# Where LayerNorm's inverse root is computed: a power on GpSimd, or a logarithm and an exponential on ScalarE

## The chip, the cores and the metric

The kernel runs on one core of a Trainium2 chip. A core has five engines that run side by side, each with its own queue of instructions taken in order: TensorE (PE; its weight loads are PEld), VectorE (DVE), ScalarE (ACT), GpSimd (POOL) and SyncE (SP), which here starts the DMA transfers. An instruction that needs what another engine makes waits for a semaphore, and all that stands behind it on its engine waits too. The metric is the time of one execution on the device, in microseconds (us), lower is better; the median of several runs is compared.

## The reference, cut to what matters

Two transformer layers with adaptive layer norm act on `x` of 16 sequences, 512 tokens and 256 channels. Each layer is a token mixer and a channel mixer, each behind a LayerNorm that is scaled and shifted per sequence, and each added back through a gate:

```python
def _layernorm(x, axis=-1, eps=1e-05):
    m = jnp.mean(x, axis=axis, keepdims=True)
    v = jnp.var(x, axis=axis, keepdims=True)
    return (x - m) / jnp.sqrt(v + eps)
...
    h = _layernorm(x, axis=-1) * (1 + ca) + sa
    x = x + ga * _L0_attn_ref(h, ...)          # fast weights: a recurrence over chunks of 16 tokens
    h = _layernorm(x, axis=-1) * (1 + cb) + sb
    x = x + gb * _L0_ffn_ref(h, ...)           # low-rank MLP with GELU
    ...
    h = _layernorm(x, axis=-1) * (1 + ca) + sa
    x = x + ga * _L1_attn_ref(h, ...)          # attention in a window of 64, and 4 global keys
    h = _layernorm(x, axis=-1) * (1 + cb) + sb
    x = x + gb * _L1_ffn_ref(h, ...)           # channel mix: squared ReLU, gated by a sigmoid
```

So there are four LayerNorms for every token. The change bears on 1 / sqrt(v + eps) in each.

## The kernel before, in words

**Units.** The 16 sequences are split in two halves of 8, and the 512 tokens in 8 blocks of 64. A half and a block make a unit, 16 in all, and the two halves take turns. A unit is a tile `x` of 128 partitions (two sequences of 64 tokens) by 4 rows of 256 channels.

**Stages.** Each unit goes through five generators: `prepare` (norm `a`, projections, convolutions and SiLU, the results spilled to memory), `chain` (the recurrence of the fast weights, four chunks of 16 tokens in a unit, `recur`), `mlp` (the end of the fast weights, then `low_rank_ffn` with norm `b` and GELU), `attend` (`window_attention` with norm `c`) and `mix` (`channel_mix` with norm `d`). The letters stand in the names of tiles: `mv_a`, `rs_a`, `off_a` and `xn_a` belong to the norm of `prepare`.

**The order of work.** The function `timetable` gives each step of each generator a due time, and the steps of all units are emitted in order of it, so five stages of several units are interleaved. A scheduler then plans, from its own estimates, the order in which each engine takes its instructions; the program is fixed before it runs. Bursts of tanh, SiLU and GELU on ScalarE go through `run`, which keeps a burst together where it can and then loads the table of the logarithm and exponential again (L234). That table, `natural_log_exp_and_others`, is the resident one between bursts.

**The recurrence.** In `recur`, VectorE makes scores from tokens and state (`sc_k`, `sc_v`, L527, and their sums, L528), ScalarE takes exponentials (L542, L613), VectorE normalises (L547 to L549, L619 to L623), GpSimd makes outer products of 128x1024 (`pd_o`, `pd_i`, `pd_kv`, L534 and L661), and VectorE sums them (L636) or scans them (L631). The state lies in PSUM. The two halves' recurrences run side by side, and a chunk starts from the state that the last one left.

**The norm.** `norm_T` (L340 on) is called 64 times, once per stage and unit:

- VectorE: statistics of each of 4 rows, `bn_stats` and `bn_aggr` (L347, L348), into `mv`, mean and variance of 128 x 4 tokens;
- GpSimd: variance plus eps (L350), and that to the power -0.5 (L351, with `mhalf`, a constant of -0.5), into `rs`;
- VectorE: `off` = -mean x `rs` (L353);
- ScalarE: `xn` = x times `rs` plus `off`, one activation for each row (L359);
- TensorE transposes `xn` (L361) into `pt`, and ScalarE scales and shifts it out of there, eight activations of 128x64 for every two rows (L367), into `hT`.

So each norm goes from VectorE to GpSimd, back to VectorE, and on to ScalarE. What stands behind `off` on VectorE and behind `xn` on ScalarE waits with them. Other places take inverse roots by logarithm and exponential on ScalarE already (`inverse_root`, L203 and L204), on tiles of 128x32.

Of the kernel before, what the change touches and what calls it, by code (L numbers as in the profile page):

```python
# [12 lines left out]
AF = mybir.ActivationFunctionType  # L13
ALU = mybir.AluOpType
# [3 lines left out]
P = 128  # L18
# [5 lines left out]
NR = HB // 2  # L24
# [10 lines left out]
EPS = 1e-5  # L35
# [60 lines left out]
def adaln_blocks(ctx: ExitStack, tc: tile.TileContext, a: dict, out: bass.AP):  # L96
    nc = tc.nc
    mul, add, sub = ALU.mult, ALU.add, ALU.subtract
# [9 lines left out]
    def ctile(shape, name):  # L108
        return const.tile(shape, F32, tag=name, name=name)

    def bank(name):
        return ps.tile([P, 512], F32, tag="bank", name=name)
# [75 lines left out]
    nc.vector.tensor_copy(ident_bf, ident)  # L188

    w_proj = ctile([P, 2, 2, C], "w_proj")  # L190
    mhalf = ctile([P, 1], "mhalf")
    nc.vector.memset(mhalf, -0.5)

    def hold(dst, n):

# [144 lines left out]
    def norm_T(x, layer, which, b0, tag, hT):  # L340


        m = mods[layer]
        mv = work.tile([P, NR, 2], F32, tag=f"mv_{tag[0]}", name=f"mv_{tag}", bufs=1)
        for r in range(NR):
            st = work.tile([P, 6], F32, tag="st", name=f"st_{tag}_{r}", bufs=4)
            nc.vector.bn_stats(st, x[:, r, :])  # L347
            nc.vector.bn_aggr(mv[:, r, :], st)  # L348
        rs = work.tile([P, NR], F32, tag=f"rs_{tag[0]}", name=f"rs_{tag}", bufs=1)
        nc.gpsimd.tensor_scalar(rs, mv[:, :, 1], EPS, None, add)  # L350
        nc.gpsimd.tensor_tensor(rs, rs, mhalf.to_broadcast([P, NR]), ALU.pow)  # L351
        off = work.tile([P, NR], F32, tag=f"off_{tag[0]}", name=f"off_{tag}", bufs=1)
        nc.vector.scalar_tensor_tensor(off, mv[:, :, 0], -1.0, rs, mul, mul)  # L353
        for r2 in range(NR // 2):
            pt = bank(f"pt_{tag}_{r2}")
            for n in range(2):
                r = 2 * r2 + n
                xn = work.tile([P, C], F32, tag="xn", name=f"xn_{tag}_{r}", bufs=2)
                nc.scalar.activation(xn, x[:, r, :], AF.Identity, scale=rs[:, r : r + 1], bias=off[:, r : r + 1])  # L359
                for k in range(2):  # L360
                    nc.tensor.transpose(pt[:, (2 * n + k) * P : (2 * n + k + 1) * P], xn[:, k * P : (k + 1) * P], ident)  # L361
            for n in range(2):
                for k in range(2):
                    for e in range(2):
                        b = 4 * r2 + 2 * n + e
                        col = (2 * n + k) * P + e * TB
                        nc.scalar.activation(  # L367
                            hT[:, k, b, :],
                            pt[:, col : col + TB],
                            AF.Identity,  # L370
                            scale=m[:, 2 * which + 1, k, b0 + b : b0 + b + 1],
                            bias=m[:, 2 * which, k, b0 + b : b0 + b + 1],
                        )
            yield
# [35 lines left out]
    def prepare(u):  # L410
# [7 lines left out]
        x = load_x(u, f"xa{u}", "xa", 1)  # L418
        hT = hidden("a", f"hTa{u}")
        yield from norm_T(x, 0, 0, b0, f"a{u}", hT)  # L420
        hf = [hT[:, k].rearrange("p b t -> p (b t)") for k in range(2)]

# [295 lines left out]
    def low_rank_ffn(i, x):  # L718
        b0 = place(i)[0] * HB
        hT = hidden("b", f"hTb{i}")  # L720
        yield from norm_T(x, 0, 1, b0, f"b{i}", hT)
        pp = bank(f"pP{i}")
        for k in range(2):
# [46 lines left out]
    def window_attention(i, x):  # L770
# [4 lines left out]
        far, last = tb > 1, tb == T // TB - 1  # L775
        hT = hidden("c", f"hTc{i}")
        yield from norm_T(x, 1, 0, b0, f"c{i}", hT)
        hf = [hT[:, k].rearrange("p b t -> p (b t)") for k in range(2)]

# [415 lines left out]
```

## Time and profile before

| | before |
|---|---|
| median of 3 runs | 3226.88 us (3222.9 to 3235.52) |
| the profiled execution | 3231.29 us, of which the span from first to last instruction 3229.5 us |
| VectorE busy | 2395.3 us, 4513 instructions |
| TensorE busy (ends modelled) | 2385.4 us, 17232 matmuls |
| ScalarE busy | 1783.6 us, 3748 instructions, 232 of them table loads of 1283 ns |
| GpSimd busy | 1673.0 us, 1575 instructions |
| granted TensorE clock | 0.822 of full speed |

The profile is of one execution. "Busy" counts an instruction from its start to its end. A row of a group reads: line, engine, operation, the tile written and the tiles read, shape, how often; then busy us and the mean ns of one; then the idle time of the engine just before these instructions and what ended it. The chain of waits is followed back from the last instruction, at each step to what released it.

### The profile page before, as it was taken

How to read it: one execution, taken by the hardware profiler on the slowest of the kernel's cores; microseconds unless marked ns; L12 is line 12 of the kernel's file. 1: busy time of each engine (PE TensorE's matmuls, PEld its weight loads, DVE VectorE, ACT ScalarE, POOL GpSimd, SP SyncE). 2: the span in 40 equal slices, each digit the busy share in tenths (PEclk: the TensorE clock that was granted, in tenths of full speed). 3: DMA queues.
4: the chain of work that ended last, by engine and by line, in shares of the span. 5: the costliest groups of instructions: out<-in, count | busy, mean ns of one | idle time of the engine just before them, and what ended most of it. 6: DMA issues, size and time to landing. Idle time of an engine off the chain costs nothing.

```text
span 3229.5 us, 47324 instructions
## 1 busy us (share of the span) xinstructions
PE 2385.4 (74%) x17232; PEld 1452.9 (45%) x17232; DVE 2395.3 (74%) x4513; ACT 1783.6 (55%) x3748; POOL 1673.0 (52%) x1575
## 2 busy tenths in 40 slices
PE   3540156868787776887788887889787888788996
PEld 2210123444444454554445554555445555555664
DVE  1688787878787787778888888888888878774221
ACT  1761354556665745565564666566664655445543
POOL 0245556556556655555556564555555655654112
PEclk7775676878797887888888798979888887879998
DMA  5420112132314132131313223230402212122010
GB/s 151 94 58 13 47 37 67 31 73 55 80 36 94 32 83 54 51 83 33 88 27 72 69 59 75 51 83 27 100 21 72 62 51 56 45 52 60 17 28 27
DMA packets 439307, 186.46 MB, mean 58 GB/s; under 512 B 323937, under 2 KB 413090, under 8 KB 439074
## 3 DMA queue, kind: packets, MB, share of 16 engines
q1 hardware_dynamic: 439074, 183.44, 23.2%
q8 instruction: 135, 2.21, 0.3%
q14 instruction: 98, 0.80, 0.1%
HBM read 116.66 MB, written 66.72 MB: 57 GB/s over the span
## 4 chain that ended last, share of the span: by engine, by line
DVE 33%; PE 22%; POOL 20%; ACT 12%; issue 8%; DMA 4%; SPq 1%; POOLq 0%; DVEq 0%; ACTq 0%
POOL pd_o L534 5%; POOL pd_i L534 4%; DVE pd_kv L631 4%; DVE sc_v L527 3%; POOL pd_kv L534 3%; DVE sv L528 3%; DVE do L636 2%; PE st L873 2%; DVE di L636 2%; DVE sc_k L527 2%; DVE pp L460 2%; PE pproj L1005 2%; DMA oT<-o 2%; DVE scs L528 2%; DVE mx L889 1%
## 5 line engine op out<-in xcount | busy, mean ns | idle before, releaser
L534 POOL TENSOR_TENSOR pd_o<-e_k,dt_v 128x1024 f32<-128x1024 f32 x128 | 301.0, 2358 | 171.4 <-DVE e_k L549 171.3
L534 POOL TENSOR_TENSOR pd_i<-e_v,dt_k 128x1024 f32<-128x1024 f32 x128 | 298.4, 2369 | 43.4 <-DVE e_v L549 43.4
L708 PE MATMUL pwo<-w_WoT,oT 128*128 128x256 f32 x256 | 106.6, 576 | 223.0 <-POOL oT L701 201.8
L873 PE MATMUL st<-qs,keys 32*128 32x128 f32 x2048 | 191.3, 336 | 71.7 <-DVE yT L983 29.0
L661 POOL TENSOR_TENSOR pd_kv<-hid,pd_kv 128x1024 f32<-128x1024 f32 x64 | 150.3, 2349 | 165.6 <-DVE fw L632 141.6
L873 PE MATMUL sc<-keys,qs 32*128 32x128 f32 x2048 | 183.1, 326 | 71.7 <-DVE mx L889 41.7
L636 DVE TENSOR_REDUCE do<-pd_o 128x64 f32<-128x1024 f32 x126 | 152.3, 1213 | 102.5 <-POOL pd_o L534 102.5
L636 DVE TENSOR_REDUCE di<-pd_i 128x64 f32<-128x1024 f32 x128 | 155.1, 1214 | 88.3 <-POOL pd_i L534 88.3
L873 PEld LDWEIGHTS st<-qs,keys 32*128 32x128 f32 x2048 | 160.5, 226 | 132.2 <-DVE mx L889 32.4
L873 PEld LDWEIGHTS sc<-keys,qs 32*128 32x128 f32 x2048 | 148.0, 216 | 141.9 <-DVE mx L889 58.8
L889 DVE TENSOR_REDUCE mx<-sc 128x4 f32<-128x512 f32 x256 | 168.2, 679 | 26.2 <-PE sc L870 26.2
L708 PEld LDWEIGHTS pwo<-w_WoT,oT 128*128 128x128 f32 x256 | 68.4, 287 | 250.7 <-POOL oT L701 218.3
L534 POOL TENSOR_TENSOR pd_kv<-hid,dt_v 128x1024 f32<-128x1024 f32 x64 | 151.4, 2366 | 54.7 <-DVE hid L623 50.0
L926 ACT ACTIVATE pT<-st 128x512 f32<-128x512 f32 x256 | 135.3, 605 | 73.7 <-PE st L870 73.4
L631 DVE TENSOR_TENSOR_SCAN pd_kv<-within,pd_kv 128x1024 f32<-128x1024 bf16 x64 | 174.4, 2725 | 0.9
L527 DVE TENSOR_TENSOR sc_k<-tok,fw 128x1024 f32<-128x1024 f32 x128 | 155.4, 1214 | 14.8 <-ACT tok L597 13.5
L527 DVE TENSOR_TENSOR sc_v<-tok,fw 128x1024 f32<-128x1024 f32 x128 | 150.3, 1215 | 1.6
L224 ACT ACT_TABLE_LOAD x111 | 142.4, 1283 | 14.3 <-PE ph L736 7.6
L528 DVE TENSOR_REDUCE sv<-sc_v 128x64 f32<-128x1024 f32 x128 | 149.6, 1209 | 0.0
L736 PE MATMUL ph<-PT,w_v 64*128 64x512 f32 x256 | 111.1, 669 | 38.0 <-ACT z L224 27.8
L1005 PE MATMUL pproj<-w_proj,yT 128*128 128x256 f32 x512 | 122.9, 386 | 11.2 <-DVE yT L983 9.3
L197 PE MATMUL pmx<-w_w_attnT,blocks 128*128 128x384 f32 x256 | 118.5, 593 | 13.4 <-ACT hp L367 9.4
(251 smaller groups left out, 6827.7 us busy)
## 6 DMA issues: line engine op xcount, KB each, us to landing
values<-values SPq DMA_DIRECT2D x56, 256.0 KB
gate_a<-gates SPq DMA_DIRECT2D x64, 128.0 KB
xa<-in_x_dram SPq DMA_DIRECT2D x32, 256.0 KB
x<-in_x_dram SPq DMA_DIRECT2D x32, 256.0 KB
gate_c<-gates SPq DMA_DIRECT2D x64, 128.0 KB
gate_d<-gates SPq DMA_DIRECT2D x64, 128.0 KB
q<-y SPq DMA_DIRECT2D x64, 128.0 KB
dt_q<-q SPq DMA_DIRECT2D x32, 256.0 KB
```

Of the source, the lines that this page charges most:

```text
L224: ins = nc.scalar.activation(*args[0], **args[1])
L527: engine.tensor_tensor(pr, tok.unsqueeze(1).to_broadcast(every), w.unsqueeze(2).to_broadcast(every), mul)
L528: nc.vector.tensor_reduce(dst, pr, AX.X, add)
L534: engine.tensor_tensor(pr, hid.unsqueeze(2).to_broadcast(every), tok.unsqueeze(1).to_broadcast(every), mul)
L631: nc.vector.tensor_tensor_scan(flat, within, flat, 0.0, mul, add)
L636: nc.vector.tensor_reduce(t, pr, AX.X, add)
L661: nc.gpsimd.tensor_tensor(po, qh.unsqueeze(2).to_broadcast([P, R, D, CH]), upto, mul)
L708: nc.tensor.matmul(po[:, n * C : (n + 1) * C], lhsT=pair(oT, k, 2 * b2 + n), rhs=w_o[:, k, :], start=k == 0, stop=k == 1,)
L873: nc.tensor.matmul(dst, lhsT=lhsT, rhs=rhs, start=start, stop=False, skip_group_check=True)
L889: nc.vector.tensor_reduce(mx[:, j], sc[j].rearrange("p (s k) -> p s k", s=NS), AX.X, ALU.max)
L926: nc.scalar.activation(pT[j], st[j], AF.Exp)
L1005: nc.tensor.matmul(po[:, n * C : (n + 1) * C], lhsT=yT[:, k2, par].rearrange("p e t -> p (e t)"), rhs=w_proj[:, k2, par, :], start=k2 == 0 ...
```

## The change

The root is no longer made by GpSimd. ScalarE takes the logarithm of variance plus eps, with eps as the activation's bias from a constant tile, and then the exponential of -0.5 times that. The constant tile `mhalf` goes and `eps` comes, one memset each. All else in the source is the same; the scheduler plans the engines' orders anew.

```diff
-    mhalf = ctile([P, 1], "mhalf")
-    nc.vector.memset(mhalf, -0.5)
+    eps = ctile([P, 1], "eps")
+    nc.vector.memset(eps, EPS)
...
         rs = work.tile([P, NR], F32, tag=f"rs_{tag[0]}", name=f"rs_{tag}", bufs=1)
-        nc.gpsimd.tensor_scalar(rs, mv[:, :, 1], EPS, None, add)
-        nc.gpsimd.tensor_tensor(rs, rs, mhalf.to_broadcast([P, NR]), ALU.pow)
+        nc.scalar.activation(rs, mv[:, :, 1], AF.Ln, bias=eps)
+        nc.scalar.activation(rs, rs, AF.Exp, scale=-0.5)
         off = work.tile([P, NR], F32, tag=f"off_{tag[0]}", name=f"off_{tag}", bufs=1)
         nc.vector.scalar_tensor_tensor(off, mv[:, :, 0], -1.0, rs, mul, mul)
```

## The prediction, made before the result was known

> **What bounds the kernel now.** I read the page's busy shares and its chain first, then the busy time by stretches, then the groups of the changed lines, and last the time line around single norms.
>
> ```profile
> PE 2385.4 (74%) x17232; PEld 1452.9 (45%) x17232; DVE 2395.3 (74%) x4513; ACT 1783.6 (55%) x3748; POOL 1673.0 (52%) x1575
> ...
> DVE 33%; PE 22%; POOL 20%; ACT 12%; issue 8%; DMA 4%; SPq 1%; POOLq 0%; DVEq 0%; ACTq 0%
> ```
>
> ```profile
> 1627.00:1815.00 188.00, 155.09 (x1079) 94.12 (x1069) 154.85 (x286) 110.95 (x228) 104.75 (x101) 0.83 0.25 60
> 1815.00:1992.00 177.00, 151.93 (x1222) 93.00 (x1224) 150.89 (x280) 113.03 (x245) 100.64 (x97) 0.88 0.26 64
> ```
>
> The second fence is the busy time by stretches: start and end, length, then busy us of PE, PEld, DVE, ACT and POOL. These are two of the sixteen units' periods. VectorE works 155 of 188 and 151 of 177 us, 83 to 85%; nothing else that has to keep its order is as full (a busy TensorE in these rows is modelled and pipelined). VectorE takes its instructions in order, so a period is its work plus its waits. The chain hops between it and GpSimd, whose outer products (L534) answer it. A wait of VectorE on GpSimd is therefore the dearest kind, and the changed lines make one in every norm:
>
> ```profile
> L353 DVE SCALAR_TENSOR_TENSOR off_a<-mv_a,rs_a 128x4 f32<-128x4 f32 x16 | 15.8, 988 | 16.4 <-POOL rs_a L351 16.4
> L353 DVE SCALAR_TENSOR_TENSOR off_c<-mv_c,rs_c 128x4 f32<-128x4 f32 x16 | 13.4, 837 | 23.6 <-POOL rs_c L351 23.6
> L353 DVE SCALAR_TENSOR_TENSOR off_b<-mv_b,rs_b 128x4 f32<-128x4 f32 x16 | 9.1, 566 | 5.4 <-POOL rs_b L351 5.4
> L353 DVE SCALAR_TENSOR_TENSOR off_d<-mv_d,rs_d 128x4 f32<-128x4 f32 x16 | 9.0, 565 | 25.3 <-POOL rs_d L351 25.3
> ...
> L351 POOL TENSOR_TENSOR rs_d<-rs_d,mhalf 128x4 f32<-128x4 f32 x16 | 16.6, 1036 | 1.3
> L350 POOL TENSOR_SCALAR rs_d<-mv_d 128x4 f32<-128x4 f32 x16 | 3.7, 229 | 12.8 <-DVE mv_d L348 12.8
> ```
>
> These are groups of instructions: busy us and mean ns of one, then the engine's idle us before them with its cause. VectorE stands idle 16.4 + 23.6 + 5.4 + 25.3 = 70.7 us before the 64 `off`. And `off` itself is odd: four numbers a partition, median 164 ns by its rows, yet a mean of 565 to 988. The time line shows why (start us, length us; VectorE, then GpSimd):
>
> ```profile
> 1262.09 2.28 DVE L353 SCALAR_TENSOR_TENSOR off_a<-mv_a,rs_a 128x4 f32<-128x4 f32 x1 [1.30 <-POOL rs_a L351]
> ...
> 1261.02 1.04 POOL L351 TENSOR_TENSOR rs_a<-rs_a,mhalf 128x4 f32<-128x4 f32 x1
> 1262.03 2.32 POOL L534 TENSOR_TENSOR pd_kv<-hid,dt_v 128x1024 f32<-128x1024 f32 x1
> ```
>
> The power ends, GpSimd goes straight on with the outer product that queued behind it, and `off`, which starts 0.06 us later, ends only with that product. It happened 18 times, 36.7 us over the median. So 70.7 + 36.7 = 107.4 us of VectorE hang on these lines. The chain of waits tells the same for one norm:
>
> ```profile
> 1201.10 0.21 POOL rs_d L350
> 1201.31 0.07 issue
> 1201.38 1.04 POOL rs_d L351
> 1202.42 0.02 issue
> 1202.45 0.16 DVE off_d L353
> 1202.61 1.14 DVE sc_k L527
> ```
>
> The recurrence's scores (`sc_k`) wait 1.5 us for a norm of another stream. Summed over the whole chain, L350 and L351 stand in it with 59.7 us (44 of 64 norms) and `off` with 24.8: 84.5 us.
>
> **The change part by part.** *Removed from GpSimd:* 64 additions and 64 powers, 20.4 us + 66.8 us = 87 us by their rows (one addition took 2.1 us, else 0.23 + 1.04). Beyond the 70.7 us that VectorE waited, about half of the powers had an outer product queued right behind them, which now starts some 1.3 us earlier.
>
> *Added to ScalarE:* 64 logarithms and 64 exponentials on 128x4. The nearest rows are the same pair on 128x32 (L203, L204):
>
> ```profile
> L203 ACT ACTIVATE ov<-ov 128x32 f32<-128x32 f32 x32 | 6.6, 226 | 22.7 <-DVE ov L679 22.6
> L204 ACT ACTIVATE ov<-ov 128x32 f32<-128x32 f32 x32 | 6.5, 221 | 0.0
> L224 ACT ACT_TABLE_LOAD x111 | 142.4, 1283 | 14.3 <-PE ph L736 7.6 <-PE pQ L743 4.8
> ```
>
> 64 x (0.226 + 0.221) = 28.6 us. [...] The latency from statistics to root falls from 0.09 + 1.35 to about 0.1 + 0.45 us where ScalarE is free. Both functions are in the set that is resident between bursts, but when one falls into a burst of tanh, SiLU or GELU it costs loads: the built program has 236 loads, 232 before. Four at 1.283 us by the row are 5.1 us. [...] ScalarE is 55% busy and stood idle 169 us before the first `xn` of the norms; that idle time is the cover of these 34 us. Without it they would all be added.
>
> *The wait that replaces the old one.* `off` now waits for ScalarE, where the logarithm queues behind copies and bursts. The order of the built program says how much. In it `off` stands eight or more VectorE instructions behind the last statistics in 34 norms, against 5 before, and at most two behind in 14, against 41. I took for each norm, from the trace of before, the end of the ScalarE instruction that now stands ahead of the logarithm, 0.55 us for the pair, and the end of the VectorE instruction that now stands ahead of `off`. The positive differences sum to 41.7 us, against 70.7. Of it 26.4 come from three norms (`a` of unit 10, `c` of units 8 and 10) whose statistics themselves moved, so that the old times don't fit. Ends: 15 and 42 us; I take 20, near the low end, since those three should resemble their neighbours. Freed: 51 us.
>
> *The collisions.* [...] By the rows of four other small or middling VectorE instructions with two SBUF inputs (L573, L679, L900, L1033), 44 of 176 ran long, 48.7 us over their medians, 0.28 each: 18 us. I take 20 of the 36.7 as staying. Freed: 17 us.
>
> *The sum.* 51 + 17 = 68 us of VectorE's time, a little under the 84.5 of the chain. Not all passes to the end, for a wait removed lets the next begin earlier. VectorE's largest other waits are for GpSimd's products (102.5 + 88.3 + 22.2 = 213 us, which move with it, or sooner) and for ScalarE and TensorE (92.4 + 57.2 + 44.0 + 29.2 + 28.6 + 26.2 + 21.8 + 21.5 = 321 us, which need not move). By that split 40% passes; by the busy share, 82%. I take 0.6: 41 us. Against it 3 us for the table loads and for activations that fall where ScalarE is in the chain. Net 38 us: 3231.3 of the profiled execution (span 3229.5 and 1.8 around it) less 38 is 3193. The median of the runs stands 4.4 us under that execution, so 3189, 1.2% below 3226.9.
>
> *What moves besides.* VectorE's and TensorE's orders change in many places, SP's in some (the gate loads go ahead of or behind loads of x), as the scheduler replans. I cost that at nothing, with 15 us either way; DMA engines are 23% busy. In the first units one half of `xn_a` now stands behind two SiLU bursts, some 6 us later, covered by the chain already running there.
>
> **The rivals.** *Absorbed.* The next wait takes all but 10 us: 3217 to 3227, taken as 3220. For it: `do` waiting for `pd_o` and `yT` for `rs` are each larger than the norms' wait. Against: GpSimd itself is relieved.
>
> *ScalarE's queue becomes the bound (slower).* ScalarE is in order too. A logarithm at its head waits for statistics, then `xn` waits for an `off` that stands later on VectorE, and behind both queue the recurrence's exponentials (L542, L613: 256 in all), for which VectorE waits before L547 and L549. By the same reading of neighbours, ScalarE's waits at these places are 81 us before logarithms and 157 before `xn`, 238 against 169 now: 69 more, plus 34 of added work, 103. If 70% lands on the path, that is +72 - 41 = +31: 3258. It decides above 0.40 (41 of 103). Against: many of these waits fall where ScalarE had nothing else to do, as the order puts the recurrence's exponentials around them.
>
> *The order as planned isn't what runs.* Where `off` meets a late ScalarE (the `d` norms of u = 5 to 10, whose logarithm follows 13 us of backlog) VectorE waits as before. If all 64 kept their old wait, only the collisions and GpSimd's time would be gained: 3217, inside the first rival.
>
> **How the numbers follow.** The forecast 0.52, with its own range 3160 to 3210 (all 107 us with 0.6, or 40% of 68, and the 15 us of reordering); absorbed, or cancelled by the reordering, 0.21; ScalarE's queue 0.27, spread 3244 to 3285. This kernel's measurement tells about 0.5% from no change, that is 3211 to 3243. The forecast's case gives faster with 0.51 of its 0.52, the absorbed case 0.03 of faster, 0.16 of same and 0.02 of slower; the queue 0.02 of same and 0.25 of slower, the rest of the forecast being same: faster 0.54, same 0.19, slower 0.27. The range leaves out the far tails of both sides: 3150 to 3262.
>
> **What would show it.** Right: VectorE's idle before L353 at 15 to 45 us and now released by ScalarE; fewer `off` near 2.3 us, some 20 us of excess; GpSimd's busy time near 1586; ScalarE's near 1817 with 236 loads; L353 almost gone from the chain, and the periods some 2 to 3 us shorter. Wrong: periods unchanged while VectorE's idle before L636, L983 or L1033 grows by what L353 lost; or, for the queue, VectorE idle before L547, L549 and L619 and ScalarE idle before L350 of 80 us and more.

## The result, and the profile after

| | before | after |
|---|---|---|
| median of 4 runs each, same chip | 3228.6 us (3222.9 to 3235.52) | 3189.35 us (3188.57 to 3195.17) |
| ratio, 95% interval | 1 | 0.9881 (0.9858 to 0.9905) |
| span of the profiled execution | 3229.5 us | 3186.8 us |
| VectorE busy, and span less busy | 2395.3, 834.2 us | 2392.2, 794.6 us |

The kernel is 1.2% faster, 39 us by the medians and 42.7 us by the two spans. On the page of the kernel after, the busy shares and the shares of the chain:

```profile
PE 2368.4 (74%) x17232; PEld 1450.8 (46%) x17232; DVE 2392.2 (75%) x4513; ACT 1809.4 (57%) x3880; POOL 1588.0 (50%) x1447
...
DVE 36%; PE 21%; POOL 18%; ACT 12%; issue 8%; DMA 4%; SPq 1%; POOLq 0%; DVEq 0%; ACTq 0%
```

GpSimd lost 85 us of work, ScalarE gained 26, and VectorE has the same instructions to do. Of the 42.7 us, 39.6 are VectorE's idle time and 3.1 its busy time. The groups of the norm, and below them four groups of VectorE that come up again:

```profile
L353 DVE SCALAR_TENSOR_TENSOR off_a<-mv_a,rs_a 128x4 f32<-128x4 f32 x16 | 6.2, 385 | 0.6 <-ACT rs_a L351 0.6
L353 DVE SCALAR_TENSOR_TENSOR off_c<-mv_c,rs_c 128x4 f32<-128x4 f32 x16 | 4.8, 298 | 0.1
L353 DVE SCALAR_TENSOR_TENSOR off_d<-mv_d,rs_d 128x4 f32<-128x4 f32 x16 | 3.3, 203 | 10.2 <-ACT rs_d L351 10.2
L353 DVE SCALAR_TENSOR_TENSOR off_b<-mv_b,rs_b 128x4 f32<-128x4 f32 x16 | 2.4, 151 | 0.6 <-ACT rs_b L351 0.6
...
L350 ACT ACTIVATE rs_d<-mv_d,eps 128x4 f32<-128x4 f32 x16 | 4.8, 298 | 9.2 <-DVE mv_d L348 9.2
L351 ACT ACTIVATE rs_d<-rs_d 128x4 f32<-128x4 f32 x16 | 3.2, 203 | 0.3
L224 ACT ACT_TABLE_LOAD x115 | 147.5, 1283 | 15.9 <-PE ph L736 10.0 <-PE pQ L743 4.2
...
L636 DVE TENSOR_REDUCE do<-pd_o 128x64 f32<-128x1024 f32 x126 | 152.5, 1214 | 123.2 <-POOL pd_o L534 123.2
L631 DVE TENSOR_TENSOR_SCAN pd_kv<-within,pd_kv 128x1024 f32<-128x1024 bf16 x64 | 186.4, 2912 | 0.8
L900 DVE TENSOR_TENSOR mx<-mx,mg 128x16 f32<-128x16 f32 x48 | 30.8, 642 | 0.4
L573 DVE SCALAR_TENSOR_TENSOR lr<-lr,lrt 128x64 f32<-128x64 f32 x32 | 20.9, 655 | 10.3 <-ACT lrt L210 10.2
```

VectorE's idle time before `off` fell from 70.7 to 11.5 us (the last column of the first four rows), and the excess of `off` over its median (0.164 us before, 0.153 after) from 36.8 to 6.8: 89 us less at this line. But VectorE's idle time before `do` grew by 20.7 (it was 102.5), and three groups that the change doesn't touch became longer. In the kernel before they read:

```profile
L631 DVE TENSOR_TENSOR_SCAN pd_kv<-within,pd_kv 128x1024 f32<-128x1024 bf16 x64 | 174.4, 2725 | 0.9
L900 DVE TENSOR_TENSOR mx<-mx,mg 128x16 f32<-128x16 f32 x48 | 20.4, 426 | 0.4
L573 DVE SCALAR_TENSOR_TENSOR lr<-lr,lrt 128x64 f32<-128x64 f32 x32 | 14.1, 444 | 10.8 <-ACT lrt L210 10.8
```

That is 12.0 + 10.4 + 6.8 = 29.2 us more for the same work, as much as `off` no longer loses to GpSimd's outer products. The long ones of these three groups run beside work of GpSimd too: with none beside them, L631, L900 and L573 took at most 2.29, 0.19 and 0.23 us, before and after. Those of L631 stand mostly beside outer products (15 before, 20 after), those of L573 only beside shorter instructions (`dt_k` and `dt_q`, 1.3 us). So the collisions moved and didn't go; what remains is idle time, 59.2 us less at `off` and 20.7 more at `do`.

The busy time by stretches, at the same clock times as the two stretches that the prediction showed:

```profile
1627.00:1815.00 188.00, 153.34 (x1171) 93.95 (x1170) 157.02 (x286) 115.98 (x249) 100.43 (x92) 0.87 0.25 62
1815.00:1992.00 177.00, 148.05 (x1099) 92.47 (x1099) 146.79 (x270) 108.64 (x230) 91.76 (x84) 0.84 0.26 62
```

The faster kernel is further along by then, so these stretches hold somewhat other work (1171 and 1099 matmuls, not 1079 and 1222), and the rows can't be compared one by one. The periods can: from the last statistics of one norm `b` to those of the next, ten periods took 176 to 191 us before, and of these eight are 3 to 6 us shorter and two are 7 and 9 longer, 21 us less in all. The other half of the gain lies ahead of them and behind.

### The profile page after: what moved, and what is told of

Read it like the earlier page. It is cut to its first block, busy times and chain, and to the rows that moved or that the text cites. A ratio compares the mean times of both kernels' runs of the same rounds, so it can differ in the third digit from the quotient of the medians.

```text
span 3186.8 us, 47321 instructions
## 1 busy us (share of the span) xinstructions
PE 2368.4 (74%) x17232; PEld 1450.8 (46%) x17232; DVE 2392.2 (75%) x4513; ACT 1809.4 (57%) x3880; POOL 1588.0 (50%) x1447
## 4 chain that ended last, share of the span: by engine, by line
DVE 36%; PE 21%; POOL 18%; ACT 12%; issue 8%; DMA 4%; SPq 1%; POOLq 0%; DVEq 0%; ACTq 0%
POOL pd_o L534 5%; DVE pd_kv L631 5%; POOL pd_i L534 4%; DVE sc_v L527 4%; DVE sv L528 3%; POOL pd_kv L534 3%; PE pproj L1005 2%; DVE do L636 2%; DVE di L636 2%; DVE mx L889 2%; DVE scs L528 2%; DVE sc_k L527 2%; PE ph L736 1%; DMA oT<-o 1%; POOL x L389 1%
## 5 line engine op out<-in xcount | busy, mean ns | idle before, releaser
L534 POOL TENSOR_TENSOR pd_i<-e_v,dt_k 128x1024 f32<-128x1024 f32 x128 | 297.1, 2358 | 54.5 <-DVE e_v L549 54.5
L636 DVE TENSOR_REDUCE do<-pd_o 128x64 f32<-128x1024 f32 x126 | 152.5, 1214 | 123.2 <-POOL pd_o L534 123.2
L631 DVE TENSOR_TENSOR_SCAN pd_kv<-within,pd_kv 128x1024 f32<-128x1024 bf16 x64 | 186.4, 2912 | 0.8
L224 ACT ACT_TABLE_LOAD x115 | 147.5, 1283 | 15.9 <-PE ph L736 10.0
L1005 PE MATMUL pproj<-w_proj,yT 128*128 128x256 f32 x512 | 124.4, 387 | 11.5 <-DVE yT L983 9.7
L197 PE MATMUL pmx<-w_w_attnT,blocks 128*128 128x384 f32 x256 | 111.6, 563 | 7.9 <-DVE up_a L387 3.1
```

The source lines that it names most:

```text
L224: ins = nc.scalar.activation(*args[0], **args[1])
L534: engine.tensor_tensor(pr, hid.unsqueeze(2).to_broadcast(every), tok.unsqueeze(1).to_broadcast(every), mul)
L631: nc.vector.tensor_tensor_scan(flat, within, flat, 0.0, mul, add)
L636: nc.vector.tensor_reduce(t, pr, AX.X, add)
L1005: nc.tensor.matmul(po[:, n * C : (n + 1) * C], lhsT=yT[:, k2, par].rearrange("p e t -> p (e t)"), rhs=w_proj[:, k2, par, :], start=k2 == 0 ...
```

## The experiments

The change does three things at once. The root goes to ScalarE, GpSimd is rid of 128 instructions, and the scheduler, which plans from other costs, puts the instructions of all engines in another order. Below, *order B* is the order of the kernel before and *order A* that of the kernel after. Where a kernel is said to stand in one of them, every engine takes all other instructions in that order; only those that make a root differ. In the traces they do, but for two of 64 spare pairs of one run that stand up to five places off. It is done with edges between neighbours that are declared without a semaphore (`NoSync`):

```diff
+def pin(tc, nc):
...
+    for order in plan.values():
...
+        for first, then in zip(order, order[1:]):
+            tc.add_manual_dep(
...
+        adaln_blocks(tc, aps, out)
+        pin(tc, nc)
```

Each ratio is to the kernel before, run beside it on the same chip; its median there was 3232 to 3234 us. It is not always the quotient of the two medians (0.9943 and 0.9952 in one case below, 1.0003 and 0.9992 in another). No run holds an order and changes nothing else; the nearest, with an unread addition in order A (0.9875) and an unread pair in order B (1.0013), leave the edges themselves little to cost.

### Order or root

My theory was the prediction's: `off` stands later on VectorE, and that frees the time. The rival: the root's way through GpSimd's queue is what costs, wherever `off` stands. First the old root in order A: the norm of the kernel before, and the pin with the other order.

> The root stays a power on GpSimd, but every other instruction of all five engines stands in the order of the changed kernel (edges that fix the order, no waits). Theory of the prediction (VectorE no longer waits for the root at `off`, GpSimd is relieved of 87 us): `off` stands late, so most of VectorE's 71 us of idle before it goes, but the powers still hold up outer products: about 3205, half of the gain. Rival A (all of it is the new order): 3190, as the changed kernel. Rival B (all of it is GpSimd's 87 us and the shorter path): 3225 to 3240, no gain.

Measured: 1.0022 (1.0006 to 1.0038). Then the new root in order B: the change's diff, and the pin with the order of the kernel before.

> The root is made by logarithm and exponential on ScalarE, but every other instruction of all five engines stands in the order of the kernel before. `off` follows the statistics closely again, in 41 of 64 norms within two instructions. Theory of the prediction: GpSimd is relieved and the path is some 0.9 us shorter where ScalarE is free, but VectorE waits where ScalarE has a backlog: about 3210. Rival A (all of it is the new order): 3228 or more, no gain. Rival B (GpSimd's work and the path): 3190.

Measured: 0.9874 (0.9854 to 0.9895). As a square:

| | order B | order A |
|---|---|---|
| root on GpSimd | 1 | 1.0022 |
| root on ScalarE | 0.9874 | 0.9881 |

The order as a whole is worth nothing with either root (0.2% worse with the old one, no resolved difference with the new one), and the root is worth all of it in both. What the place of `off` alone is worth is not shown, since the order moves much else with it. The groups of `off` show how little its idle time says. Order A with the root on GpSimd:

```profile
L353 DVE SCALAR_TENSOR_TENSOR off_c<-mv_c,rs_c 128x4 f32<-128x4 f32 x16 | 7.6, 476 | 5.5 <-POOL rs_c L351 5.5
L353 DVE SCALAR_TENSOR_TENSOR off_a<-mv_a,rs_a 128x4 f32<-128x4 f32 x16 | 6.2, 388 | 5.1 <-POOL rs_a L351 5.1
L353 DVE SCALAR_TENSOR_TENSOR off_d<-mv_d,rs_d 128x4 f32<-128x4 f32 x16 | 2.5, 159 | 4.5 <-POOL rs_d L351 4.4
L353 DVE SCALAR_TENSOR_TENSOR off_b<-mv_b,rs_b 128x4 f32<-128x4 f32 x16 | 2.5, 156 | 2.7 <-POOL rs_b L351 2.7
```

Order B with the root on ScalarE:

```profile
L353 DVE SCALAR_TENSOR_TENSOR off_c<-mv_c,rs_c 128x4 f32<-128x4 f32 x16 | 11.2, 697 | 11.9 <-ACT rs_c L351 11.9
L353 DVE SCALAR_TENSOR_TENSOR off_a<-mv_a,rs_a 128x4 f32<-128x4 f32 x16 | 9.7, 607 | 12.0 <-ACT rs_a L351 12.0
L353 DVE SCALAR_TENSOR_TENSOR off_d<-mv_d,rs_d 128x4 f32<-128x4 f32 x16 | 7.9, 495 | 13.9 <-ACT rs_d L351 13.9
L353 DVE SCALAR_TENSOR_TENSOR off_b<-mv_b,rs_b 128x4 f32<-128x4 f32 x16 | 2.5, 156 | 15.5 <-ACT rs_b L351 15.4
```

In the first, VectorE's idle time is down to 17.8 us and its collisions to 9, and the kernel is no faster than before. In the second VectorE still stands idle for 53.2 us and collides for 21, and the kernel has the whole gain. With the order held, VectorE's loss at `off` fell by 33 us in it (107.6 to 74.3) and the span by 39.7. ScalarE's wait for `off` before `xn` says more. For norm `c`, in the kernel before, in order B with the root on ScalarE, in order A with the root on GpSimd, and in the kernel after:

```profile
L359 ACT ACTIVATE xn_c<-x,off_c,rs_c 128x256 f32<-128x256 f32 x64 | 36.3, 622 | 52.9 <-DVE off_c L353 49.1 <-DVE mv_d L348 2.7 <-PE pt_c L361 1.1
L359 ACT ACTIVATE xn_c<-x,off_c,rs_c 128x256 f32<-128x256 f32 x64 | 36.0, 618 | 23.0 <-DVE off_c L353 13.6 <-DVE mv_d L348 8.3 <-PE pt_c L361 1.0
L359 ACT ACTIVATE xn_c<-x,off_c,rs_c 128x256 f32<-128x256 f32 x64 | 35.9, 617 | 53.7 <-DVE off_c L353 41.5 <-DVE mv_d L348 11.6 <-PE pt_c L361 0.6
L359 ACT ACTIVATE xn_c<-x,off_c,rs_c 128x256 f32<-128x256 f32 x64 | 35.9, 617 | 25.8 <-DVE off_c L353 18.4 <-DVE mv_d L348 6.6 <-PE pt_c L361 0.6
```

For all four norms it falls with the root from 153.6 to 63.4 us in order B, and from 170.3 to 116.6 in order A.

### The way or the work: is it that the root comes sooner, or that GpSimd has less to do?

The new root stays, and the old pair is still made on GpSimd, at the old root's place in its queue, into a tile that nobody reads. This is extra work that doesn't bear on the output. In order A:

```diff
         nc.scalar.activation(rs, rs, AF.Exp, scale=-0.5)
+        spare = work.tile([P, NR], F32, tag=f"spare_{tag[0]}", name=f"spare_{tag}", bufs=1)
+        nc.gpsimd.tensor_scalar(spare, mv[:, :, 1], EPS, None, add)
+        nc.gpsimd.tensor_tensor(spare, spare, mhalf.to_broadcast([P, NR]), ALU.pow)
```

> The changed kernel, every instruction of all five engines in its order, and besides the old addition and power on GpSimd in each norm, into a tile that nothing reads: GpSimd is as busy as before (87 us more), and nobody waits for the result. Theory now (GpSimd's occupation is what cost: the products queued behind each power start some 1.3 us later): 3225 to 3240, all of the gain gone. Rival D (the shorter path from statistics to `xn` is what gained): 3187 to 3200, the gain stays.

Measured: 0.9943 (0.9924 to 0.9961), between the two expectations, so about half of the gain is gone, 0.62% or 20 us, although no one waits for these results. A stretch of its chain (start us, length us; this kernel's lines stand 5 lower in the recurrence) shows how:

```profile
1515.99 0.15 POOL tails L461
1516.13 0.21 POOL spare_c L355
1516.34 0.07 issue
1516.41 1.04 POOL spare_c L356
1517.45 2.31 POOL pd_o L539
1519.77 0.02 issue
1519.79 1.22 DVE do L641
```

The spare power delays the outer product behind it, and `do` on VectorE waits for that. Over the run the waits show it:

```profile
DVE do L641 <- POOL pd_o L539: 141.0, 68, 6.3
```

The same wait is 123.2 us in the kernel after. With the addition alone (its 64 places are the old ones too, and it still stops the queue until the statistics are there: at 1240.17 us, in its chain, it starts 0.08 us behind them), in order A:

```diff
+        nc.gpsimd.tensor_scalar(spare, mv[:, :, 1], EPS, None, add)
```

> The changed kernel in its own order, with the old addition alone on GpSimd in each norm, into a tile that nothing reads: 15 us of GpSimd's time instead of 87, but GpSimd's queue still stops for the statistics of each norm. If it is the length of the power that costs: 3190 to 3203, some 15 of 87 of the difference. If it is that GpSimd's queue stops for the statistics: 3215 to 3230.

Measured: 0.9875 (0.984 to 0.9909), no different from the kernel after within this interval, and clear of the run with the pair. So it is not the stop for the statistics; it is the power's 66 us.

Then the wait by itself. Both roots are made, as in the kernel with the spare pair, and `off` reads GpSimd's, while `xn` takes its scale from ScalarE's:

```diff
-        nc.vector.scalar_tensor_tensor(off, mv[:, :, 0], -1.0, rs, mul, mul)
+        nc.vector.scalar_tensor_tensor(off, mv[:, :, 0], -1.0, spare, mul, mul)
```

> The run in the changed kernel's order with the unused power on GpSimd, with one edit: `off` takes its root from that power, while `xn` still takes it from ScalarE. GpSimd's and ScalarE's work and all orders are as in that run; only the wait goes through GpSimd's queue again. If the later root is what the other half of the gain came from: 3235 to 3250, as the run with the power in the changed order (1.0022) or some 5 us above it, since ScalarE's pair is made as well. If GpSimd's queue was no slower a way than ScalarE's: 3210 to 3222 (0.9943, as without the edit).

Measured: 1.0003 (0.999 to 1.0016), another 0.60% or 19 us. VectorE's idle time at `off` rises by only 7.7 us for it (10.1 to 17.8), that of ScalarE at `xn` for `off` by 14 (122.1 to 136.3). So in order A the gain has two parts, the work and the way, and both are clear of noise. Their sizes are known less well: with the intervals of the ratios, taken as independent, 20 us is good to some 10 and 19 to some 7, and the quotients of the medians would give 24 and 13.

In order B the same question has another answer. The change's root in order B, with the old pair kept unread on GpSimd:

> The root on ScalarE in the order of the kernel before, and the old addition and power kept on GpSimd into a tile that nothing reads: GpSimd's occupation alone, in the other order. If the two halves found in the changed order hold here as well: 3208 to 3220 (0.9925 to 0.9965). If GpSimd's occupation costs nothing in this order, as its second dose did (1.0013 on 1): 3190 to 3200. If it is all of it: 3228 and more.

Measured: 0.9882 (0.9867 to 0.9897). Of the 1.26% of order B, 1.18 are there with all of GpSimd's work in place, and the 0.08% left for the work are not resolved. And the other way round, the kernel before with a second addition and power behind the first, in order B:

> The kernel before in its own order, with a second addition and power in each norm on GpSimd into a tile that nothing reads: twice the dose, 87 us more than before. Theory now (GpSimd's occupation): 3255 to 3285, about as much slower as the change was faster. Rival D (the path): 3228 to 3240.

Measured: 1.0013 (1.0002 to 1.0024). Twice the work costs 0.13%, 4 us for 79 us more on GpSimd. Here is a reason that I had not thought of, in two of its groups:

```profile
L356 DVE SCALAR_TENSOR_TENSOR off_c<-mv_c,rs_c 128x4 f32<-128x4 f32 x16 | 2.6, 161 | 24.8 <-POOL rs_c L351 24.7
L356 DVE SCALAR_TENSOR_TENSOR off_a<-mv_a,rs_a 128x4 f32<-128x4 f32 x16 | 2.6, 161 | 17.8 <-POOL rs_a L351 17.7
```

`off_c` took 837 ns on average in the kernel before, `off_a` 988, and both take 161 here. When the root is ready, GpSimd now starts another small power and not an outer product, and `off` runs free of collision: 60 of the 64 run beside the second power. VectorE's busy time falls by 29 us (2395.3 to 2365.9), which pays for `do`, whose wait grows from 102.5 to 126.1, and for most of the 36 us by which VectorE's idle time grows in all.

Why does the work cost 20 us in order A and some 3 in order B? The traces suggest an answer that no run tests. In both, the spare pair makes VectorE wait longer for `pd_o`: 123.2 to 141.0 us in order A, 102.1 to 117.2 in order B. In order B `off` follows close behind, with 53.2 us of idle time and 21.1 us of collisions to take that up, and they fall to 42.1 and 13.4. In order A `off` has only 11.5 us to give, and gives 1.4.

### ScalarE's side

The change, and a second logarithm and exponential behind the first into an unread tile; here the scheduler plans anew:

```diff
         nc.scalar.activation(rs, rs, AF.Exp, scale=-0.5)
+        nc.scalar.activation(spare, mv[:, :, 1], AF.Ln, bias=eps)
+        nc.scalar.activation(spare, spare, AF.Exp, scale=-0.5)
```

> The changed kernel with the logarithm and exponential made twice in each norm, the second pair into a tile that nothing reads: 32 us more on ScalarE. Planned anew. Theory of the prediction (ScalarE's own idle time covers its new work): 3186 to 3196. Rival C (ScalarE's queue is a bound and the change wins in spite of it): 3205 or more.

Measured: 0.9899 (0.9879 to 0.9919), 0.18% above the kernel after with intervals that overlap: some 6 us, not resolved, for 32 us of added work by its rows. ScalarE's busy time grows by 13.5 us only (1809.4 to 1822.9). I put that down to overlap in the records, where a time covered twice counts once: in the kernel after, 2467 of ScalarE's records start before the one ahead of them ends, by 115 ns on average. Most of the added work is covered.

If GpSimd's queue is the place to be relieved, more might be moved. The kernel after, with four small copies moved from GpSimd to ScalarE (L453, L456, L1025, L1028: 56 us in 224 instructions on GpSimd), planned anew:

```diff
-                    nc.gpsimd.tensor_copy(xp[:, :, 0:3], tg)
+                    nc.scalar.copy(xp[:, :, 0:3], tg)
...
-                    nc.gpsimd.tensor_copy(tg, xp[:, :, TB:])
+                    nc.scalar.copy(tg, xp[:, :, TB:])
...
-                nc.gpsimd.tensor_copy(hp[:, k, :, 0:1], hlast[:, k, bs, :])
+                nc.scalar.copy(hp[:, k, :, 0:1], hlast[:, k, bs, :])
...
-                nc.gpsimd.tensor_copy(hlast[:, k, bs, :], hp[:, k, :, TB:])
+                nc.scalar.copy(hlast[:, k, bs, :], hp[:, k, :, TB:])
```

> The changed kernel with its small copies of convolution tails and last tokens (84 + 84 + 28 + 28 instructions, 54 us on GpSimd) on ScalarE as well. Planned anew. If GpSimd's occupation costs about half of its length on the path and ScalarE's a fifth, as the run with the doubled pair has it: 15 to 25 us faster than the changed kernel, 3165 to 3178. Rival: these copies wait for ScalarE or feed VectorE in other places and were in nobody's way: 3185 to 3200.

Measured: 0.9988 (0.9973 to 1.0004), outside both expectations. The whole gain is gone. The order is new as well here, and no run holds it, so what follows is read from the waits and not tested. ScalarE's queue took over what these copies wait for. Its waits (engine, tile and line, releaser, us in total, times, longest):

```profile
ACT xp L453 <- DVE y L460: 73.7, 16, 9.9
ACT hp L1025 <- PE pkv L1079: 73.4, 12, 10.3
```

and VectorE's, in the same kernel:

```profile
DVE yT L983 <- ACT rs L979: 119.4, 24, 13.2
DVE di L636 <- POOL pd_i L534: 98.0, 60, 3.4
DVE do L636 <- POOL pd_o L534: 93.7, 62, 3.0
DVE ss_q L579 <- ACT sq_q L558: 67.7, 14, 8.0
```

`do` waits 30 us less than in the kernel after, as hoped, and `di` 12 more. But `yT` waits 119.4 and not 85.6, and `ss_q` 67.7 and not 28.6. A copy that waits 5 or 6 us at the head of ScalarE's queue (73.7 us in 16 waits, 73.4 in 12) holds up every activation behind it, those of the recurrence included. As I read it, this is the prediction's slower rival, brought about by another edit.

### `off` on GpSimd

Is it VectorE's wait at `off` that must go? The kernel before, with `off` on GpSimd too, so that VectorE neither makes it nor waits for it; planned anew:

```diff
-        nc.vector.scalar_tensor_tensor(off, mv[:, :, 0], -1.0, rs, mul, mul)
+        nc.gpsimd.tensor_tensor(off, mv[:, :, 0], rs, mul)
+        nc.gpsimd.tensor_scalar(off, off, -1.0, None, mul)
```

> The kernel before with `off` made on GpSimd too, as a product and a sign change right behind the power; VectorE has then neither a wait nor an instruction between the statistics and the next work. Planned anew. Theory of the prediction (VectorE's wait is what cost): VectorE loses 71 us of idle and 47 us of busy time while GpSimd gains some 35 us of work: 3180 to 3205. Rival B (GpSimd's work is what cost): 3240 to 3260, slower than before.

Measured: 1.0103 (1.0078 to 1.0129), slower than either expectation. VectorE is rid of the 107 us, 2341.7 us busy, and yet idle for 928. ScalarE now waits for GpSimd before it can make `xn`:

```profile
L360 ACT ACTIVATE xn_a<-xa,off_a,rs_a 128x256 f32<-128x256 f32 x64 | 36.9, 606 | 92.2 <-POOL off_a L354 84.6 <-PE pt_a L362 7.3
L360 ACT ACTIVATE xn_c<-x,off_c,rs_c 128x256 f32<-128x256 f32 x64 | 35.9, 608 | 55.2 <-POOL off_c L354 53.9 <-PE pt_c L362 1.4
```

With the other two norms it is 216 us of waiting for `off`, against 154 in the kernel before. VectorE's wait for `e_v` (before L548 there) is 45 us, against 5 in the kernel before (at L547), and I read it so that this exponential stands behind those `xn`; the order is new here too, and no run holds it.

### One table

The chain's time on the root (the spare pair too) and `off`, summed over the whole chain by the tiles' names; VectorE's idle time before `off` and before `do`; ScalarE's idle time before `xn` for `off`; all us.

| order, root | ratio | chain on root and `off` | idle before `off` | before `do` | before `xn` |
|---|---|---|---|---|---|
| A, ScalarE (after) | 0.9881 | 13.9 | 11.5 | 123.2 | 116.6 |
| A, and the old addition unread | 0.9875 | 17.4 | 11.9 | 126.2 | 114.4 |
| A, and the old pair unread | 0.9943 | 32.7 | 10.1 | 141.0 | 122.1 |
| A, and `off` reads the old pair | 1.0003 | 53.9 | 17.8 | 136.3 | 136.3 |
| A, GpSimd | 1.0022 | 54.5 | 17.8 | 137.4 | 170.3 |
| B, ScalarE | 0.9874 | 38.2 | 53.2 | 102.1 | 63.4 |
| B, and the old pair unread | 0.9882 | 42.0 | 42.1 | 117.2 | 50.6 |
| B, GpSimd (before) | 1 | 84.4 | 70.7 | 102.5 | 153.6 |
| B, GpSimd, and a second pair unread | 1.0013 | 104.7 | 77.1 | 126.1 | 150.6 |

Within one order the chain column goes with the ratio. In order A its two large steps are 18.8 and 21.3 us on the chain, and 20 and 19 by the ratios; in order B 3.8 and 42.4, and 3 and 38. The second pair doesn't fit, 20 on the chain for 4. This agreement is not to be leaned on to the microsecond: the chain is that of one profiled execution, and in order A the spans of the profiled executions step by 29.5 and 4.9 us, for the execution profiled where `off` reads the old pair was the fastest of its 12. In order B they step by 1.0 and 38.7. The idle time before `off` follows nothing. Between the orders no column holds, since a new order moves other waits as well: after and before differ by 70.5 on the chain and by 39 in time.

## Why the prediction was right in its number and wrong in its reason

The forecast was 3189, and the time is 3189.35. That it fits so closely is luck, as the steps show:

- **"`off` stands eight or more VectorE instructions behind the last statistics in 34 norms", freeing 51 us.** This step failed. The idle time did fall, and by more than I said (to 11.5, not 20). But the new order, with that place in it, is not what brought the time: with it and the old root nothing is gained (1.0022), and without it and with the new root all is (0.9874). I took the wait as gone when VectorE no longer stood in it. In truth a root on GpSimd had to pass through a queue of outer products of 2.3 us, and `xn`, the transposes and `hT` wait for it wherever `off` stands: with the old root in order A, ScalarE still idles 170 us before `xn` for `off`. On ScalarE the root is ready, by the median, 1.04 us after the last statistics in order A and 0.67 in order B, against 2.92 before. The means differ less, 2.82, 1.69 and 2.81 us (3.10 with the old root in order A): in the kernel after, six norms get their root only 12 us after their statistics, behind other work of ScalarE.
- **"The latency from statistics to root falls from 0.09 + 1.35 to about 0.1 + 0.45 us."** This stood in the prediction as a remark under the costs of ScalarE and entered no sum. It was half of the gain in order A and nearly all of it in order B, and by the median larger than I wrote, since 1.35 us left out the queue.
- **"Beyond the 70.7 us that VectorE waited, about half of the powers had an outer product queued right behind them."** I named GpSimd's relief and gave it no price. In the order that runs it is worth 20 us, about half of the gain. The remark itself was loose: by the trace some instruction follows at once behind 31 of the 64 powers, but an outer product behind 21.
- **The collisions: 17 of 36.7 us freed.** At `off` 30 us went, and 29 came back at L631, L900 and L573. There are as many outer products as before (384, of 2.36 us on average before and 2.35 after), and VectorE's work is the same; I counted collisions for `off` alone. The 20 us that I took as staying there was an estimate near the 18 by the rows of other instructions; 6.8 stayed in the kernel after, and 21 in order B with the new root. The 29 us came with the new order and not with the root: order A with the old root has 186.4, 25.4 and 20.6 us at the three lines, and order B with the new root 174.5, 20.9 and 14.6, much as before. VectorE's whole busy time fell by 3.1 us, so this term was 14 us too high.
- **"I take 0.6" as what passes.** Of 59.2 us of idle time and 3.1 of busy time, 42.7 came through, 0.68. But `do` took 20.7 us back, and by the square of orders and roots this quotient is no property of the wait. That two of my terms (51 us for the place, 17 for the collisions) came out as 62 together, while neither cause was the one that brought the time, is why the number fits.
- **ScalarE's cost, 3 us.** The logarithm took 298 to 311 ns, the exponential 203 to 215: 64 pairs are 32.6 us by their rows, against 28.6 by the rows without a bias. The rest of ScalarE's rows are 12 us shorter than before, so its busy time is 1809.4 and not 1817. The 236 loads stayed at 1283 ns. What of it shows at the end is about 6 us by the doubled pair, twice my 3, with intervals that overlap.
- **The rivals.** "Absorbed" is excluded by the interval. "ScalarE's queue becomes the bound" did not come: ScalarE idles 40 us before the logarithms (11.7 + 6.2 + 12.6 + 9.2) and 127 before the first `xn` of the norms, against my 81 and 157. My reading of neighbours took the old times for the new order, and with the root coming sooner the neighbours moved too. The four copies suggest that the mechanism exists, and that four lines which wait for late results are enough.

## What to carry to other kernels

A wait on an in-order queue is to be priced by what its result passes through and who needs it at the end, not by the idle time of the engine that happens to stand in it (here 53.2 us of it before `off` went with the whole gain, and 17.8 with none); hold the order and change the cause, or hold the cause and change the order, before you credit either. A small instruction in the queue of an engine that the critical recurrence answers to can cost time even if nobody reads its result (20 us for 87 us of pairs in order A), or nearly nothing (3 and 4 us in order B), by what waits behind it. When work is moved between queues, ask first what each moved instruction waits for: the logarithm's statistics came mostly in time (39.7 us of waiting for all 64) and its move cost little, the copies' inputs came late (73.7 and 73.4 us at two of the lines) and the whole gain went with them.

## What the runs showed of the hardware that I had not expected

- Collisions between VectorE and GpSimd can move instead of going: in the kernel after, 30 us less of them at `off` came with 29 us more at three other lines. It is no law, for in order B the same root took 17 us off VectorE's busy time (2395.3 to 2378.2), and the three lines kept their times. At these lines they go with the order.
- A power of 128x4 on GpSimd, 1.04 us, does not hold up a 128x4 `off` beside it (162 ns on average in 60 cases), while an outer product does, up to 2.3 us. Work put between the root and the product pays back part of its own cost, 29 us of VectorE's busy time here.
- A logarithm of 128x4 with a bias from a tile took 298 to 311 ns, the exponential behind it with none 203 to 215; the pair on 128x32 took 226 and 221 before.
